# Two graph layers with their edge stages in a written-out order, and the router's and features' work laid beside other stages

## The chip, the cores and the metric

The kernel runs on one core of a Trainium2 chip. The metric is device time in microseconds (us) from launch to end, lower is better. A core has five engines that run side by side, each through its own queue in order: PE (matrix products, results into PSUM), DVE (vector work), ACT (activation functions and copies), POOL (here mostly gathers by index, which it issues as DMAs) and SP (plain DMAs). They wait for each other by semaphores.

## The reference

Two rounds over one graph of 3125 nodes (256 features) and 53,125 edges, each round followed by a feed-forward part. Cut to what matters:

```
x1 = layernorm(x);  feats[h] = x1 @ Ws[h] + bs[h]                      # 4 heads of 64
w  = exp(-relu((a_s[src] + a_d[dst] + aw_e*elem + ab) / 20))           # per edge, head
x += segment_sum(w * feats[dst], src) / segment_sum(w, src)            # edge stage 0
x2 = layernorm(x);  x += sum over the top 2 of 16 experts of p_e * expert_e(x2)
h  = layernorm(x);  score = h[src]@w_src + h[dst]@w_dst + rel[etype]@w_rel
al = exp(leaky_relu(score)); al = al / al
agg = segment_sum(((h[src] + rel[etype]) @ Wn) * al, dst)              # edge stage 1
x += relu(agg) + where(in_degree > 0, h @ loop_w, h @ evolve_w)
z  = layernorm(x);  wt = z @ wr + br                                   # one number per node
x  = x + z + (the 1561 nodes of highest wt: wt * (gelu(z@w1 + b1)@w2 + b2))
```

All products are in float32; indicator matrices are bf16 or f16.

## The kernel before, in words

The nodes are 25 tiles of 128. A sort in the kernel (`sort_edges`) puts the edges into 25 buckets by the node that receives, 18 tiles of 128 edges a bucket (8 in the last), 440 tiles in all. The sort for round 0 comes first; the ranking part of the sort for round 1 is a Python generator whose pieces are given as `fill` to edge stage 0, and its moves are spread over the experts.

An edge stage (`edge_stages`, run by `pipelined`) goes over 74 groups of up to 6 edge tiles, three groups to a bucket. `gather` lets POOL fetch a row of the table per edge into `rows` (L754), builds the one-hot `oh` of the receiving node (DVE, L762) and the transposed one-hots `hot` (DVE, L771) from `wide`, a bucket's row numbers broadcast to all partitions by a DMA on SP (L744). `message` multiplies `hot` by the nodes' own parts (PE, `ps_near`, L780; 6 products a group in stage 0, 18 in stage 1), adds the pieces (DVE, L787) and calls `messages`: in stage 0 two exponentials on ACT (L924, L925) and the product of weights and rows (DVE, L926); in stage 1 the edge's weight (L1310 to L1282), the relation's one-hot written beside the row (DVE, L1313) and six scaled copies of `oh` on ACT (L1319). `add` sums over the edges by products with `oh` into the bucket's PSUM half (PE, L798). At a bucket's end `acc` takes the sum plus `more`, loaded just then from DRAM (L804, L806), and `finish` ends the bucket: in stage 0 a division and the sum into `x` (L937 to L940), then `done`, which every five buckets normalizes and makes the gate's logits; in stage 1 four transposes and eight products on PE (L1330 to L1343), copies on ACT and seven operations on DVE.

The order of instructions on each queue is not the program's: the framework's planner reorders what stands in different steps by its own costs. Products of all kinds but the sums and the experts' hidden layer share the four PSUM buffers of `ps_b`.

After edge stage 0 come the experts (65 tiles of 128 rows, weights streamed per tile), the sum of the experts' results into `x` over 25 tiles with two gathers each (L1170, L1174), then `relations_features`: weights for the relations, layer norm of all tiles (`norm_tiles`), features of all tiles into `table1` (L1264 to L1270). Then edge stage 1, then `depths`: layer norm of all tiles, the score `wc`, its transposed copy `wrow`, the rank of every node by comparing with all others (49 comparisons, `cmp`, L1426), and the last feed-forward part tile by tile (L1445 to L1473).

Of the kernel before, what the change touches and what calls it, by code (L numbers as in the profile page):

```python
# [9 lines left out]
F32 = mybir.dt.float32  # L10
# [12 lines left out]
class _Kernel:  # L23
# [12 lines left out]
    def __init__(self, ctx, tc, a, out):  # L36
# [18 lines left out]
        for b in range(self.NT):  # L55
# [7 lines left out]
        assert self.MT % self.KB == 0  # L63
# [3 lines left out]
        self.psum = ctx.enter_context(  # L67
            tc.tile_pool(name="psum", bufs=1, space=bass.MemoryType.PSUM)
        )
# [5 lines left out]

    def ps_a(self, name):
        return self.psum.tile([P, 1024], F32, tag="A", name=name, bufs=2)

    def ps_b(self, name):
        return self.psum.tile([P, 512], F32, tag="B", name=name, bufs=4)  # L80
# [17 lines left out]
    def constants(self):  # L98
# [14 lines left out]
        iota_i = self.work.tile([P, 512], I32, name="iota_i", bufs=1)  # L113
        nc.gpsimd.iota(iota_i, pattern=[[1, 512]], base=0, channel_multiplier=0)
        self.iota = c.tile([P, 512], F32, name="iota")
        nc.vector.tensor_copy(self.iota, iota_i)
# [51 lines left out]
    def transposed(self, src, n, name, evac=None):  # L168

        nc, c = self.nc, n // P  # L170
        pt = self.ps_b(f"ps_{name}")
        for i in range(c):
            nc.tensor.transpose(pt[:, i * P : (i + 1) * P], src[:, i * P : (i + 1) * P], self.ident)  # L173
        dst = self.work.tile([P, c, P], F32, tag=f"T{c}", name=name, bufs=3)
        (evac or nc.scalar.copy)(dst.rearrange("p c q -> p (c q)"), pt[:, :n])  # L175
        return dst
# [133 lines left out]
    def sort_edges(self, pool, rp, name, seg, other, value, bits, tab, help, roomy):  # L310
# [23 lines left out]
        def load_in():  # L334
# [6 lines left out]
            yield  # L341
# [23 lines left out]
            yield  # L365

        def places():
# [4 lines left out]
            for b0 in range(0, NT, piece):  # L372
                m = min(piece, NT - b0)
                hot = tl([P, piece, EC], BF16, "hot", bufs=1)
                for b in range(b0, b0 + m):
                    eng = nc.vector if b % 3 == 0 else help
                    eng.tensor_scalar(hot[:, b - b0, :], bf, float(b), None, op0=OP.is_equal)
                    if b % 6 == 5:
                        yield
                hv = hot.rearrange("p b (s t) -> p b s t", t=C)  # L380
                for w, ps in ((self.ones_h, tot), (self.before_h, pre)):
# [5 lines left out]
                    yield  # L387
# [39 lines left out]
            yield  # L427
# [3 lines left out]
            for b in range(NT):  # L431
# [13 lines left out]
                yield  # L445
# [39 lines left out]
            for s in range(NS):  # L485
# [13 lines left out]
                if s % 3 == 2:  # L499
                    yield  # L500
# [77 lines left out]
        def load():  # L578
# [4 lines left out]
            wide = [self.dram.tile([MT, P], BF16, name=f"{name}_w{i}") for i in range(1 + (not bits))]  # L583
            with tc.tile_pool(name=f"{name}_back", bufs=1) as bp:
# [13 lines left out]
                def turned(v):  # L598
                    pt = self.psum.tile([P, 1024], F16, tag="B", name=f"{name}_pt", bufs=4)
# [13 lines left out]
                for i, w in enumerate(wide):  # L613
                    wb = bp.tile([P, nb, P], BF16, name=f"{name}_wb{i}")
                    nc.vector.tensor_copy(wb[:m], tk[:m, :, :, 1 + i])
                    nc.sync.dma_start(w.rearrange("(i k) p -> k i p", k=m), wb[:m])
# [107 lines left out]
    def edge_stages(self, pool, st, table, width, into, near, others, messages, W, sums, finish):  # L724
# [4 lines left out]
        nc, G = self.nc, self.GRP  # L729
        nv = near.shape[3]  # L730
        now = {}


        hold, sums2 = self.ps_a("ps_hold"), self.ps_a("ps_sums")
        numbers = hold[:, :256]
        nc.vector.tensor_copy(numbers, self.iota[:, :256])
        self.numbers, self.weights_ps = numbers, hold[:, 512:]

        def spread(i, b):

            t = pool.tile([P, self.tiles[0] // 2, 2 * P + 8], BF16, name=f"wide{i}")
            src = st["wide"][i][self.first[b] : self.first[b] + self.tiles[b], :]
            src = src.rearrange("(o k i) p -> o k (i p)", o=1, i=2)
            nc.sync.dma_start(  # L744
                t[:, : self.tiles[b] // 2, : 2 * P], src.to_broadcast([P, self.tiles[b] // 2, 2 * P])
            )
            return t

        def gather(g, b, k, n, head, last):
            if head:  # L750
                now[b] = [spread(i, b) for i in range(len(st["wide"]))]
            rows = pool.tile([P, G, into], F32, name="rows", bufs=3)
            for j in range(n):
# [5 lines left out]
                )  # L759
            sh = [P, n, P]  # L760
            oh = pool.tile([P, G, P], F32, name="oh", bufs=3)
# [4 lines left out]
            lo = (k - self.first[b]) // 2  # L766
            hots = []
            for i, (at, _) in enumerate([(self.pcol1, None)] + others):
                w = now[b][min(i, 1)][:, lo : lo + n // 2, : 2 * P]
                t = pool.tile([P, G // 2, 2 * P], BF16, name=f"hot{i}", bufs=2)  # L770
                nc.vector.tensor_scalar(t[:, : n // 2, :], w, at, None, op0=OP.is_equal)  # L771
                hots.append(t)
            return rows, oh, hots

        def message(g, b, k, n, head, last, rows, oh, hots):
            pe = self.ps_b("ps_near")
            picks = [near[:, b]] + [v for _, v in others]
            for j in range(n):
                for i, (t, v) in enumerate(zip(hots, picks)):
# [6 lines left out]
            own = pool.tile([P, G, nv], F32, name="near")  # L786
# [4 lines left out]
            return messages(k, n, rows, own, oh)  # L791

        def add(g, b, k, n, head, last, oh, msg):
            if head:
                now["sum"] = sums2[:, b % 2 * 512 : (b % 2 + 1) * 512]
            ps = now["sum"]
            for j in range(n):
                nc.tensor.matmul(  # L798
                    ps[:, :W], oh[:, j, :], msg[:, j, :],
                    start=(head and j == 0), stop=(last and j == n - 1),  # L800
                )
            if last:
                more = pool.tile([P, W], F32, name="more")
                nc.sync.dma_start(more, sums[b])  # L804
                acc = pool.tile([P, W], F32, name="acc")
                nc.vector.tensor_add(acc, ps[:, :W], more)  # L806
                finish(b, acc)

        return gather, message, add

    def pipelined(self, stages, fill=()):


        groups, done = self.edge_groups(), {}
        fill = iter(fill)
        for step in range(len(groups) + len(stages) - 1):
            if step > 2:
                next(fill, None)
            for i, stage in enumerate(stages):
                g = step - i  # L820
                if 0 <= g < len(groups):
                    done[g] = stage(g, *groups[g], *(done.pop(g, None) or ()))
        for _ in fill:
            pass
# [56 lines left out]
    def heads_edges(self, st, fill, done):  # L881
# [26 lines left out]
        with self.tc.tile_pool(name="edge0", bufs=2) as pool:  # L908
# [24 lines left out]
            def finish(b, acc):  # L933
# [7 lines left out]
                done(b)  # L941

            self.pipelined(self.edge_stages(
                pool, st, self.table0, W, W, near, [], messages, W, self.sums0, finish
            ), fill)
# [3 lines left out]
    def gate(self, pool):  # L949
# [16 lines left out]
        def done(b):  # L966
# [4 lines left out]
            self.norm_tiles(xn, t0, t1)  # L971
            nc.sync.dma_start(xv[:, t0:t1, :], xn[:, t0:t1, :])
            pl = self.ps_b("ps_logit")
            for t in range(t0, t1):
                xt = self.transposed(xn[:, t, :], D, "x_t")
                for c in range(C):
                    nc.tensor.matmul(
                        pl[:, (t - t0) * NE : (t - t0 + 1) * NE], xt[:, c, :], gw[:, c, :],
                        start=(c == 0), stop=(c == C - 1),
                    )  # L980
            nc.vector.tensor_tensor(
                self.logits[:, t0:t1, :],
                pl[:, : (t1 - t0) * NE].rearrange("p (t e) -> p t e", e=NE),
                self.gate_b[:, None, :].to_broadcast([P, t1 - t0, NE]), op=OP.add,
            )
# [3 lines left out]
    def experts(self, fill):  # L989
# [5 lines left out]
        with tc.tile_pool(name="moe", bufs=2) as pool:  # L995
# [143 lines left out]
            def turned(k):  # L1139
                w3, hid = live.pop(k)  # L1140
                live[k] = w3, self.transposed(hid, HID, "h_t")
# [25 lines left out]
            for t in range(NT):  # L1167
                for i in range(2):
# [8 lines left out]
                    )  # L1177

    def relations_features(self):
        nc, a, NT, D = self.nc, self.a, self.NT, self.D
# [13 lines left out]
        with self.tc.tile_pool(name="rel", bufs=2) as pool:  # L1196
            w3 = pool.tile([P, W3 // P, W3], F32, name="w3a", bufs=1)
            nc.sync.dma_start(w3, a["L1_gnn_W3"].rearrange("(c p) j -> p c j", p=P))
            av = pool.tile([P, W3], F32, name="av", bufs=1)
            self.row_bcast(av, a["L1_gnn_a"], W3)  # L1200
            wv = pool.tile([P, W3 // P], F32, name="wv", bufs=1)
            for c in range(W3 // P):
                nc.vector.scalar_tensor_tensor(
                    w3[:, c, :], w3[:, c, :], 1.0, av, op0=OP.mult, op1=OP.mult,
                    accum_out=wv[:, c : c + 1],
                )
# [48 lines left out]
            self.h1 = self.layer_norm("xn2")  # L1255
            t1v = self.table1.rearrange("(t p) c -> p t c", p=P)
            for t0 in range(0, NT, 5):
                f = pool.tile([P, 5, D + 2], F32, name="f1")
                n = min(5, NT - t0)
                for t in range(t0, t0 + n):  # L1260
# [8 lines left out]
                nc.vector.tensor_copy(self.near1[:, t0 : t0 + n, :], f[:, :n, D + 1 :])  # L1269
                nc.sync.dma_start(t1v[:, t0 : t0 + n, :], f[:, :n, : D + 1])  # L1270

    def relations_edges(self, st):
# [27 lines left out]
        with self.tc.tile_pool(name="edge1", bufs=2) as pool:  # L1300
# [7 lines left out]
            def messages(k, n, rows, near, oh):  # L1308
                s = pool.tile([P, 3, G], F32, name="s1")
                nc.vector.tensor_add(s[:, 0, :n], near[:, :n, 0], rows[:, :n, D])  # L1310
                weight(s[:, 1, :n], s[:, 0, :n], s[:, 2, :n])
# [4 lines left out]
                )  # L1316
                ow = pool.tile([P, G, P], F32, name="ohw", bufs=3)
# [6 lines left out]
            def finish(t, acc):  # L1324

                pt = self.ps_b("ps_cnt")
                rc = [(r0, min(P, R - r0)) for r0 in range(0, R, P)]
                ct = pool.tile([P, len(rc), P], F32, name="ct")
                for i, (r0, n) in enumerate(rc):
                    nc.tensor.transpose(  # L1330
                        pt[:n, i * P : (i + 1) * P], acc[:, R0 + r0 : R0 + r0 + n], self.ident
                    )
# [225 lines left out]
```

## Time and profile before

| | us |
|---|---|
| median of 3 runs | 2635.79 (2631.52 to 2639.92) |
| the profiled execution's own time | 2845.15 |
| its span | 2842.8 |
| PE, DVE, POOL, ACT busy | 1878.6, 1446.3, 1167.4, 390.7 |
| granted PE clock, mean | 0.822 |

The profiled execution is 209 us longer than the median of the runs, so a duration from the profile is one of that execution. In the profile a row names line, engine, operation and tile, its count, busy time and mean, and after the second bar the engine's idle time before it with what ended it. "issue" is an idle time for which the profile shows no wait; "remote" is a wait that ended with a signal that the profile ties to no recorded instruction. The ends of PE's products are modelled, not observed.

By their first and last instructions the stages are: first sort and features to 430 us, edge stage 0 from 430 to 1176, experts' choice to 1210, experts to 1717, their sum to 1790, features of round 1 and loading of the sorted edges to 1872, edge stage 1 to 2560, rank and feed-forward part to the end.

### The profile page before, as it was taken

How to read it: one execution, taken by the hardware profiler on the slowest of the kernel's cores; microseconds unless marked ns; L12 is line 12 of the kernel's file. 1: busy time of each engine (PE TensorE's matmuls, PEld its weight loads, DVE VectorE, ACT ScalarE, POOL GpSimd, SP SyncE). 2: the span in 40 equal slices, each digit the busy share in tenths (PEclk: the TensorE clock that was granted, in tenths of full speed). 3: DMA queues.
4: the chain of work that ended last, by engine and by line, in shares of the span. 5: the costliest groups of instructions: out<-in, count | busy, mean ns of one | idle time of the engine just before them, and what ended most of it. 6: DMA issues, size and time to landing. Idle time of an engine off the chain costs nothing.

```text
span 2842.8 us, 24381 instructions
## 1 busy us (share of the span) xinstructions
PE 1878.6 (66%) x7534; PEld 1126.4 (40%) x7534; DVE 1446.3 (51%) x3397; ACT 390.7 (14%) x1097; POOL 1167.4 (41%) x1198
## 2 busy tenths in 40 slices
PE   3169554854544443399999991447878778785298
PEld 0024232543433332356666660323434334343166
DVE  4876225476665343644422224445655556549721
ACT  0000010010000000100112120112222222221012
POOL 4235306576654646034411115036666666650000
PEclk9999996676666667577799996768889888898599
DMA  2000325343444433144499982254545455431000
GB/s 83 0 3 5 104 89 137 93 130 112 115 100 114 116 100 101 49 150 130 131 316 318 317 291 84 87 156 131 148 129 148 130 142 149 128 85 34 8 21 18
DMA packets 258938, 334.04 MB, mean 118 GB/s; under 512 B 30861, under 2 KB 192407, under 8 KB 258807
## 3 DMA queue, kind: packets, MB, share of 16 engines
q1 hardware_dynamic: 197527, 191.26, 21.3%
q0 software_dynamic: 51920, 132.68, 17.6%
q10 hardware_dynamic: 9360, 8.52, 0.9%
q8 instruction: 61, 1.00, 0.1%
q14 instruction: 70, 0.57, 0.1%
HBM read 298.38 MB, written 33.98 MB: 117 GB/s over the span
## 4 chain that ended last, share of the span: by engine, by line
PE 39%; DVE 14%; issue 10%; POOL 9%; another core or an unknown queue 8%; DMA 4%; ACT 1%; SPq 0%; DVEq 0%; POOLq 0%; ACTq 0%
PE ps_sums L798 10%; PE ps_h L1130 9%; POOL rows L754 9%; PE ps_y L1147 4%; PE s_mv L560 3%; DVE cmp L1426 3%; PE ps_hid L1453 3%; PE ps_out L1464 3%; DMA rows<-table,s_idx 3%; DVE msg L926 2%; DVE hot L771 2%; PE ps_x_t L173 1%; PE ps_h_t L173 1%; PE ps_f L1264 1%
## 5 line engine op out<-in xcount | busy, mean ns | idle before, releaser
L754 POOL DMA_INDIRECT rows<-table,s_idx x880 | 848.6, 964 | 725.0 <-issue 240.4
L798 PE MATMUL ps_sums<-msg,oh 128*128 128x260 f32 x880 | 306.6, 519 | 261.8 <-DVE msg L926 143.1
L798 PE MATMUL ps_sums<-rows,ohw 128*128 128x457 f32 x880 | 414.0, 616 | 62.8 <-ACT ohw L1319 54.1
L798 PEld LDWEIGHTS ps_sums<-msg,oh 128*128 128x128 f32 x880 | 226.6, 265 | 325.1 <-issue 250.1
L560 PE MATMUL s_mv<-s_hv,s_hp 128*128 128x200 f16 (+1 forms) x832 | 246.8, 472 | 89.9 <-DVE s_hv L555 89.9
L798 PEld LDWEIGHTS ps_sums<-rows,ohw 128*128 128x128 f32 x880 | 179.0, 215 | 217.5 <-issue 149.6
L1130 PE MATMUL ps_h<-w,x_t 128*128 128x512 f32 x520 | 256.1, 638 | 0.0
L771 DVE TENSOR_SCALAR hot<-wide,pcols 128x768 bf16<-128x768 bf16 (+1 forms) x296 | 175.4, 597 | 73.9 <-PE ps_near L780 63.0
L560 PEld LDWEIGHTS <-s_hp 128*128 128x128 f16 x832 | 122.1, 147 | 208.7 <-issue 180.3
L762 DVE TENSOR_TENSOR oh<-ps_hold,s_row 128x768 f32<-128x768 f32 (+1 forms) x148 | 139.9, 946 | 125.7 <-remote 73.5
L1119 POOL DMA_INDIRECT xg<-xtab,who x65 | 61.9, 952 | 345.1 <-PE ps_x_t L173 302.6
L569 POOL DMA_INDIRECT s_tab<-s_rec,s_to x130 | 147.8, 1137 | 115.1 <-ACT s_rec L566 78.9
L780 PEld LDWEIGHTS <-hot 128*128 128x128 bf16 x1760 | 70.0, 98 | 212.3 <-issue 149.2
L1136 DVE TENSOR_TENSOR hid<-hid,ps_h 128x512 f32<-128x512 f32 x65 | 44.7, 688 | 210.3 <-ACT hid L1135 204.4
L1319 ACT ACTIVATE ohw<-oh,s 128x128 f32<-128x128 f32 x440 | 136.5, 388 | 106.6 <-DVE s L1282 75.2
L1130 PEld LDWEIGHTS ps_h<-w,x_t 128*128 128x128 f32 x520 | 102.8, 209 | 105.7 <-issue 105.5
L926 DVE TENSOR_TENSOR msg<-rows,ps_hold 128x1536 f32<-128x1536 f32 x74 | 128.1, 1731 | 2.0 <-ACT ps_hold L924 1.9
L787 DVE TENSOR_REDUCE near<-ps_near 128x24 f32<-128x72 f32 (+2 forms) x148 | 29.4, 198 | 190.3 <-remote 150.2
L1147 PE MATMUL ps_y<-w,h_t 128*128 128x256 f32 x520 | 122.9, 379 | 0.7 <-ACT h_t L175 0.7
L1147 PEld LDWEIGHTS ps_y<-w,h_t 128*128 128x128 f32 x520 | 98.7, 190 | 41.7 <-issue 30.6
L545 DVE TENSOR_TENSOR s_hp<-num_p,s_pp 128x1024 f16<-128x1024 f16 x104 | 71.8, 690 | 82.8 <-PE s_mv L560 81.4
L1313 DVE TENSOR_TENSOR rows<-ps_hold,s_val 128x1200 f32<-128x1200 f32 x74 | 101.1, 1367 | 6.1 <-PE ps_sums L798 6.1
(307 smaller groups left out, 2344.2 us busy)
## 6 DMA issues: line engine op xcount, KB each, us to landing
w<-in_L_ffn_w_dram SPq DMA_DIRECT2D x195, 512.0 KB
wide<-s_w SPq DMA_DIRECT2D x72, 576.0 KB
rows<-table,s_idx POOLq DMA_INDIRECT x880
ytab<-y ACTq DMA_DIRECT2D x65, 128.0 KB
sums<-sums_z SPq DMA_DIRECT2D x5, 1142.5 KB
more<-sums SPq DMA_DIRECT2D x25, 228.5 KB
sums<-sums_z SPq DMA_DIRECT2D x5, 650.0 KB
table<-f SPq DMA_DIRECT2D x5, 650.0 KB
```

The costliest lines, as they stand in the source:

```text
L560: nc.tensor.matmul(ps[:, : NK * V], hp[:, :, j], rec[:, :, :, j].rearrange("p k v -> p (k v)"), start=(j0 + j == 0), stop=(j0 + j == C - 1),)
L569: d = nc.gpsimd.indirect_dma_start(out=tab, out_offset=bass.IndirectOffsetOnAxis(ap=to[:, i : i + 1], axis=0), in_=out[:, k * CH * V : (k ...
L754: nc.gpsimd.indirect_dma_start(out=rows[:, j, :width], out_offset=None, in_=table, in_offset=bass.IndirectOffsetOnAxis(ap=st["idx"][:, k + ...
L762: nc.vector.tensor_tensor(oh[:, :n, :], numbers[:, None, :P].to_broadcast(sh), st["row"][:, k : k + n, None].to_broadcast(sh), op=OP.is_equal,
L771: nc.vector.tensor_scalar(t[:, : n // 2, :], w, at, None, op0=OP.is_equal)
L798: nc.tensor.matmul(ps[:, :W], oh[:, j, :], msg[:, j, :], start=(head and j == 0), stop=(last and j == n - 1),)
L926: nc.vector.tensor_tensor(msg[:, :n, :HO].rearrange("p j (h o) -> p j h o", o=O), rows[:, :n, :HO].rearrange("p j (h o) -> p j h o", o=O), ...
L1130: nc.tensor.matmul(ph[:, i * HID : (i + 1) * HID], xt[:, c, :], w12[:, i, c, :], start=(c == 0), stop=(c == C - 1),)
L1147: nc.tensor.matmul(py[:, :D], ht[:, c, :], w3[:, c, :], start=(c == 0), stop=(c == HC - 1))
L1313: nc.vector.tensor_tensor(rows[:, :n, R0:], self.numbers[:, None, :R].to_broadcast(sh), st["val"][:, k : k + n, None].to_broadcast(sh), op ...
L1319: nc.scalar.activation(ow[:, j, :], oh[:, j, :], AF.Copy, scale=s[:, 1, j : j + 1])
L1426: nc.vector.tensor_scalar(cmp[:, s:e], wrow[:, s:e], w, None, op0=op, op1=OP.add, accum_out=rank[:, t, i : i + 1],)
```

## The change

- `edges` takes the place of `edge_stages` and `pipelined`. Its instructions stand in the program's order on every engine (`manual_schedule`). In step g: the row numbers of group g+2 are loaded, group g is gathered, bucket ends go on by a part, one-hots and `ps_near` of group g are made, then group g-1's near parts are read and its messages and sums are made, bucket ends go on by another part, and last comes a piece of other work from a queue (`piece(2.2)`, by nominal costs written at each `yield`).
- `ps_near`, the sums and `ps_hold` have PSUM buffers of their own (2, 2, 1); three are left for all else.
- `more` is loaded at a bucket's first group instead of its end. `wide` is loaded per group, 3 rows of 264 in one run per partition (1584 bytes) instead of 9 rows of 256 per bucket; `load` writes rows of that pitch. `rows` keeps 3 buffers in stage 0 and has 4 in stage 1, where `oh` goes from 3 to 2.
- The bucket's end in stage 1 is cut into four parts over three steps; the relation's one-hot is written in the gather's step (`prepare`).
- The work of `done` (gate) is cut into pieces. The norm, the score and the rank of the last part go into edge stage 1 as pieces (`router`): each group of up to five buckets is compared with those before it and itself, so there are 122 comparisons instead of 49, over as many columns in all.
- The weights for the relations are made ahead of the experts, and each tile's round 1 features follow as soon as its experts are summed, in groups of 4, at last 3 tiles.

```diff
-        for step in range(len(groups) + len(stages) - 1):
-            if step > 2:
-                next(fill, None)
-            for i, stage in enumerate(stages):
-                g = step - i
-                if 0 <= g < len(groups):
-                    done[g] = stage(g, *groups[g], *(done.pop(g, None) or ()))
+        with tc.manual_schedule():
+            spread(0)
+            spread(1)
+            for g in range(len(groups) + 3):
+                if g + 2 < len(groups):
+                    spread(g + 2)
+                if g < len(groups):
+                    rows = gather(g)
+                if g >= 3 and groups[g - 3][4]:
+                    closers.append(close(groups[g - 3][0]))
+                go_on()
+                if g < len(groups):
+                    live[g] = rows, *hots(g)
+                    if prepare:
+                        prepare(*groups[g][1:3], rows)
+                if 0 <= g - 1 < len(groups):
+                    message(g - 1)
+                go_on()
+                piece(2.2)
+            while closers:
+                go_on()
+            piece(1e9)
...
+                t = pool.tile([P, G // 2, 2 * P + 8], BF16, name=f"wide{i}", bufs=3)
+                src = w[k // 2 : (k + n) // 2, :].rearrange("(o k) r -> o (k r)", o=1)
...
+        def route(b):
+            if b + 1 not in ends:
+                return
+            i = ends.index(b + 1)
+            t0, t1 = ends[i - 1] if i else 0, b + 1
+            for _ in self.norm_pieces(z, t0, t1):
+                yield 1.2
...
+            for t in range(t0):
+                count(t, t0 * P, end, OP.is_gt, 3 + i)
+                if t % 3 == 2:
+                    yield 2.2
+            for t in range(t0, t1):
+                lo, hi = t * P, min(N, (t + 1) * P)
+                count(t, 0, lo, OP.is_ge, 0)
+                count(t, lo, end, OP.is_gt, 1)
...
+        general = dict(A=2, B=4)
+        at_edges = dict(near=2, sums=2, hold=1, B=3)
...
+                    self.rows_bufs, self.oh_bufs = 3, 3
                     self.heads_edges(st, ranking, self.gate(pool))
...
+                    features = self.relations_features()
+                    with tc.tile_pool(name="move1", bufs=1) as moves:
+                        self.experts([lambda f=f: f(moves) for f in steps], next(features))
+                        next(features, None)
+                    st = load()
+        with tc.tile_pool(name="route", bufs=1) as pool:
+            with self.banks(**at_edges):
+                self.router(pool)
+                self.rows_bufs, self.oh_bufs = 4, 2
+                self.relations_edges(st)
+            with self.banks(**general):
+                self.depths()
```

## The prediction

> **What bounds the kernel now.** No engine is busy over two thirds of the span, so I read the busy time by stretches first: start, length, then busy us (instructions) of PE, its weight loads, DVE, ACT, POOL, then PE's clock and the DMA share.
>
> ```profile
> 430.00:800.00 370.00, 209.64 (x856) 148.79 (x857) 231.93 (x547) 23.82 (x92) 236.38 (x234) 0.68 0.43 119
> 800.00:1176.00 376.00, 176.52 (x739) 135.45 (x737) 181.46 (x432) 28.39 (x100) 197.24 (x208) 0.68 0.37 98
> 1410.00:1710.00 300.00, 300.00 (x1125) 187.07 (x1124) 78.33 (x153) 60.29 (x102) 48.54 (x52) 0.99 0.91 301
> 1710.00:1800.00 90.00, 5.38 (x23) 3.65 (x21) 45.18 (x131) 2.78 (x4) 47.58 (x50) 0.56 0.36 111
> 1800.00:1870.00 70.00, 41.37 (x186) 29.46 (x186) 23.25 (x70) 9.30 (x25) 0.00 (x0) 0.87 0.17 56
> 1870.00:2200.00 330.00, 243.75 (x1166) 123.98 (x1166) 183.38 (x451) 80.22 (x272) 202.25 (x214) 0.84 0.54 146
> 2200.00:2560.00 360.00, 284.08 (x1327) 142.89 (x1326) 198.07 (x511) 92.01 (x316) 213.70 (x227) 0.88 0.47 126
> 2590.00:2685.00 95.00, 31.80 (x107) 20.89 (x108) 94.29 (x132) 8.40 (x12) 0.00 (x0) 0.67 0.01 3
> 2685.00:2843.00 158.00, 149.81 (x560) 100.98 (x559) 29.23 (x66) 35.15 (x58) 0.00 (x0) 0.99 0.05 19
> ```
>
> Edge stage 0 (first two rows, 746 us) has PE, DVE and POOL each near 55%: nobody is the bound, they wait in turn. Edge stage 1 (690 us) has PE at 76%. The experts are PE's and stay as they are. In 1710 to 1870 one engine works at a time; in 2590 to 2685 DVE alone; in the last row PE alone. Next, who waited for whom in stage 0 (us in total, times, longest), with one such wait in order of time (start, length, [idle before]):
>
> ```profile
> DVE oh L762 <- remote: 73.5, 9, 14.0
> DVE acc L806 <- remote: 70.8, 6, 18.4
> POOL rows L754 <- DVE msg L926: 161.5, 19, 23.6
> POOL rows L754 <- issue: 120.9, 397, 0.3
> ```
>
> ```profile
> 873.61 4.55 PE L798 MATMUL ps_sums<-msg,oh 128*128 128x260 f32 x12 [3.21 <-issue]
> 890.89 0.95 POOL L754 DMA_INDIRECT rows<-table,s_idx  x1 [0.30 <-issue]
> 895.90 0.43 DVE L806 TENSOR_TENSOR acc<-ps_sums,more 128x260 f32<-128x260 f32 x1 [16.00 <-remote]
> ```
>
> PE's record of the bucket's sums ends at 878.2, yet `acc`, which reads them, starts at 895.9; `more` for it was issued some 40 us earlier. So PE's product was signalled late (the modelled ends hide it), DVE stood with all its queue behind `acc`, freed no `rows`, and POOL stopped after filling its buffers. Such waits of DVE (`oh`, `acc`, 38.7 us more of `near`) make 183 us; 161.5 us of them reach POOL. Where the stage flows, POOL's gathers come every 0.95 + 0.30 = 1.25 us. In stage 1 PE is nearly closed:
>
> ```profile
> PE ps_near L780 <- issue: 56.1, 72, 1.9
> PE ps_sums L798 <- ACT ohw L1319: 54.1, 20, 2.8
> ```
>
> From 1885 to 2560 (675 us) PE is busy 526 us, and 85 us of its gaps are "issue" (these 56.1, and 20.1 and 8.6 before `ps_cnt` and the sums), which no reordering obviously removes. Only some 64 us are waits for others.
>
> **What the Trainium skill says.** "Perfetto Trace Analysis", section "Tensor Engine Instruction (MATMUL, LD_WEIGHTS)": the profiler computes a product's end and does not observe it; the 895.9 row agrees. "TensorE: Matmul & The Clock Gate", "What's actually happening": PE runs at half clock until it has been busy for a window. The trace agrees in direction: 0.68 in stage 0, 0.99 in the experts. "SBUF — State Buffer", "SBUF: two separate sides": DVE operations that take the shared port keep POOL from writing descriptors. The trace agrees: a gather takes 0.945 us on average in stage 1 and 0.983 in stage 0, where its longest is 1.55.
>
> **The change part by part**, in the time of the profiled execution.
>
> *Stage 0.* POOL's work stays: 440 gathers at 0.983 + 0.30 make 565 us, 7.7 a step. DVE's step in order: `hot` 0.60, `oh` 0.95, near 0.23, three small ones 0.55, a wait for ACT of about 0.35, `msg` 1.73, a bucket's end of 1.42 over three steps, together 4.9; the sort's piece (0.38 + 0.20 + 1.02 + 0.59 + 0.58) adds 2.8 in the first 40 or so steps. Consecutive DVE rows overlap by 0.1, so DVE needs 7.0 to 7.7: just under POOL. PE needs 385 us of 570. The wait is replaced by one step of slack: `near` is read a step after its products, `acc` two steps after the last sums, and `more` comes 18 tiles early. A lateness up to a step (7.7) is covered; longer ones (14 to 18 us, a handful) partly. New in DVE's strict order is that behind a late `near` stand the one-hots of the next step, which PE and ACT then wait for; I leave 20 us for these. SP issues 74 small `wide` loads at 0.36 us instead of 25; with two groups (15 us) of lead that is covered. So 565 + 15 until the first rows are used + 14 at the end + 20 = 614 against 746: **-132**.
>
> *Stage 1.* DVE: 372 us, plus two thirds of the router; the router's price: norm, score and equal-compare as now (8.2 + 15 + 8.7 + 7.8, some 40), comparisons 88.9 us for 49. The fastest took 0.277 us for 128 columns, the longest 3.47 for 3125: 1.07 ns a column and 0.14 fixed, with 0.09 for reading the sum. The 73 more comparisons cost 73 x 0.23 = 17, so 146 us, of which about 95 fall into the stage. DVE 467, POOL 440 x 1.245 = 548, PE 526 + 85 + the 25 transposes of scores (10) = 621 of 675: PE is the bound, and 8.4 us a step leave DVE's 7.7 room. SP's 148 loads and the weights that `router` now loads ahead of the stage lie beside work. **-53**. Below nothing is not excluded: a PE that rests less gets more clock; at 0.95 for 0.87 the 414 us of sums shrink by 35.
>
> *Features.* The sum over experts stays at 50 x 1.25 = 63 us of gathers, and DVE's added 25 x 1.43 = 36 us beside its 23 fit in. After the last sum (1790) there is now a norm of three tiles, three tiles of 1.87 each through PE, ACT and DVE, and the table's write: 16 us, where now the table is down at 1863. That is -57. The relations' weights (9.1 us of DMA, 5.4 + 6 of DVE) go ahead of the experts, where DVE is already busy 28 of 34 us: +12 on the path. **-45**.
>
> *End.* From 2560 to the end take 283 us now. After: the last two groups of `router` stay: for three tiles about 29 us of DVE (norm 8, 20 comparisons of 384 columns at 0.55, three of 2700 at 3.75 with company), for two tiles some 11 until their scores' copies are out, then PE can start on the feed-forward part (its buffers are handed over there); the remaining 20 of comparisons lie beside it. PE's part is 89.8 + 87.5 + 7.5 = 185, 5 to drain. 4 + 35 + 190 = 229: **-54**.
>
> The smaller edits (padded `wide` rows, two DMAs for one in `load`, `h_t` in another pool) I cost at nothing: `load` gains perhaps 2 us twice, the first `wide` (8.1 us for a bucket, seen before stage 1) comes sooner by more.
>
> Sum: -284, so the profiled execution of 2845 would become 2561. **Against the runs**: the profile is 209 us over their median, and the runs lie within 8.4 us of each other, which irregular waits of 14 to 18 us would hardly allow. So part of the late products probably is not in the runs. I take half of stage 0's gain, -66, between none and all, and the rest whole: -218, so 2635.8 - 218 = 2418, said as 2420.
>
> **The rivals.**
> 1. *The late products are in the runs as in the profile, and a steadier PE gets more clock.* For it: nothing in the records names the profiler; against it the narrow runs. -284 and up to -70: 2280 to 2370.
> 2. *The edge stages don't gain:* POOL paces stage 0 in the runs already (746 - 161 = 585, next to 565 of gathers) and PE stage 1. Only features and end: -99, or about 2535. For it: stretches such as 700 to 730, where a group took 6.9 us.
> 3. *Slower: strict order turns each late product or gather into a stop of all engines.* Place: DVE's queue in every step, `near` and the rows of g-1 ahead of the one-hots of g+1. Price: lateness beyond the step of slack. It decides from (66 + 53 + 99) / 148 steps = 1.5 us a step on; at 3 us a step it gives 2636 - 218 + 444 = 2860. Against it: gathers landed 2.5 to 5 us after issue in the chain of waits, and POOL has two more buffers to run ahead.
> 4. *The order isn't kept or changes nothing* (within 8 us of before): hardly possible with as many moved instructions.
>
> **How the numbers follow.** Forecast (2370 to 2500) 0.50, rival 1 0.22, rival 2 0.18, rival 3 0.08, rival 4 0.02. 0.3%, 8 us, is about what a measurement here can tell from no change. Faster is 0.90, same 0.02, slower 0.08. The range reaches from rival 1's all but lowest value to rival 2: 2270 to 2545.
>
> **What would show it.** In the profile after: DVE's remote waits in stage 0 under 60 us; POOL's gathers there 1.25 to 1.3 us apart with under 40 us of waits for `msg`; stage 0 near 615, stage 1 near 635 with PE busy over 80%; table 1 written within 20 us of the last expert's sum; feed-forward products within 40 us of the last bucket, without a stretch of DVE alone. It would be wrong if steps took 10 us with DVE waiting for `near` or rows in most of them, or if stage 0 were short in the profile and the runs gained under 110.

## The result, and the profile after

The changed kernel takes **2751.24 us** (median of 4 runs, 2750.01 to 2753.51) against 2635.78: ratio 1.0439, 95% interval 1.0421 to 1.0457, slower by 115 us. The prediction said 2420 and faster.

The profiled execution of the changed kernel takes 2753.51 us, like its other runs. That of before had been 209 us over its runs, so the two profiles, laid side by side, show the changed kernel 91 us *faster*. One more profile of the kernel before settled this: its own time was 2640.68, like its runs. In two of the five batches of experiments below the kernel before itself takes 2842 and 2845 us, with DVE's remote waits in the profiles of that batch, and in the other three 2635 to 2647 without them, so a ratio below is always to the kernel before of the same batch. By its time and its waits the first profile of before is like the two. Where the texts of the expectations speak of "the chip with late products", such a batch is meant, though one chip had a batch of each sort; that PE's products are what comes late is read from the waits, and why they would is open.

From here "before" is the second profile. The first view is DVE's waits in its edge stage 0, 429 to 1026 us (us in total, times, longest):

```profile
DVE s L919 <- DMA rows<-table,s_idx: 110.0, 32, 7.6
DVE near L787 <- PE ps_near L780: 35.0, 8, 7.6
DVE acc L806 <- PE ps_sums L798: 12.0, 8, 2.1
```

There is no remote wait left. DVE waits above all for gathered rows, so for POOL. By the first gather and the last `acc` of each edge stage, the spans divide so (us, to within 2; the last column is an experiment, told below, with the changed kernel's parts in the planner's order). All stage times from here on are of profiles without remote waits:

| | before | changed | planner's order |
|---|---|---|---|
| edge stage 0 | 597 | 649 | 587 |
| choice, experts, features, load | 692 | 674 | 666 |
| edge stage 1 | 636 | 763 | 572 |
| end | 284 | 235 | 216 |
| span | 2638 | 2751 | 2474 |

The changed kernel gained 67 us in the middle and at the end; the two edge stages lost 179. Busy time by stretches of the changed kernel (start, length, then busy us and instructions of PE, its weight loads, DVE, ACT, POOL, then PE's clock, DMA share, GB/s):

```profile
430.00:1077.00 647.00, 390.84 (x1585) 291.33 (x1586) 459.62 (x985) 50.81 (x190) 428.29 (x440) 0.72 0.46 126
1638.00:1762.00 124.00, 65.61 (x176) 42.25 (x177) 56.99 (x179) 12.18 (x33) 55.04 (x59) 0.52 0.39 119
1762.00:2516.00 754.00, 537.38 (x2501) 281.52 (x2497) 483.05 (x1180) 182.75 (x607) 411.15 (x433) 0.85 0.45 122
2516.00:2563.00 47.00, 8.05 (x24) 4.84 (x25) 40.72 (x113) 3.58 (x9) 0.00 (x0) 0.55 0.00 1
2563.00:2751.00 188.00, 180.18 (x669) 121.04 (x668) 49.87 (x129) 44.04 (x71) 0.00 (x0) 0.99 0.05 18
```

In edge stage 1 (third row) PE is at 71%, DVE at 64%, POOL at 55%: again nobody is the bound, and they wait in turn. For whom, waits of the changed kernel say, from 430 to 1077 (two lines) and from 1762 to 2516 (five):

```profile
DVE logits L1062 <- PE ps_logit L1059: 72.0, 23, 7.2
POOL rows L816 <- DVE msg L1002: 67.3, 15, 12.3
```

```profile
POOL rows L816 <- PE ps_sums L864: 144.9, 23, 9.2
PE ps_sums L864 <- ACT ohw L1412: 137.2, 58, 5.2
DVE agg L1447 <- PE ps_rel L1434: 124.3, 23, 6.3
DVE s L1372 <- ACT s L1371: 77.7, 73, 4.6
PE ps_near L844 <- DVE hot L830: 76.3, 82, 4.8
```

`agg` and `logits` read products of PE. In the second profile of before the same two reads wait little (1718 to 2354, and 429 to 1026):

```profile
DVE agg L1349 <- PE ps_rel L1336: 8.6, 12, 3.0
DVE logits L981 <- PE ps_logit L977: 5.7, 5, 3.0
```

One bucket's end of the changed kernel in order of time shows why (rows of PE and DVE; "..." marks rows left out):

```profile
2199.74 4.88 PE L864 MATMUL ps_sums<-rows,ohw 128*128 128x457 f32 x12 [1.10 <-ACT ohw L1412]
2204.46 1.03 PE L1434 MATMUL ps_rel<-rel_w,ct 128*128 128x257 f32 x4
2205.33 1.88 PE L1440 MATMUL ps_loop<-lw,x_t 128*128 128x512 f32 x4
2205.53 0.42 DVE L1447 TENSOR_TENSOR agg<-acc,ps_rel 128x256 f32<-128x256 f32 x1 [6.27 <-PE ps_rel L1434]
...
2208.16 1.64 DVE L830 TENSOR_SCALAR hot<-wide,pcols 128x768 bf16<-128x768 bf16 x3
2208.82 0.18 PE L844 MATMUL ps_near<-near1p,hot 128*128 128x3 bf16 x1 [1.62 <-DVE hot L830]
...
2213.71 6.60 PE L864 MATMUL ps_sums<-rows,ohw 128*128 128x457 f32 x12 [3.30 <-ACT ohw L1412]
```

`finish` issues `ps_rel` at the end of a step, behind that step's twelve products of sums (4.88 us); `agg` is the first thing that DVE does in the next step. So there is a step's *boundary* between them and no step. DVE stands 6.27 us, the next group's `hot` stands behind `agg`, and PE, done at 2207.2, waits for `hot`. ACT's scaled copies then come late, the sums start 3.30 us late, and `rows` is not freed for POOL.

### The profile page after: what moved, and what is told of

Read it like the earlier page. It is cut to its first block, busy times and chain, and to the rows that moved or that the text cites. A ratio compares the mean times of both kernels' runs of the same rounds, so it can differ in the third digit from the quotient of the medians.

```text
span 2751.4 us, 24818 instructions
## 1 busy us (share of the span) xinstructions
PE 1924.8 (70%) x7534; PEld 1165.0 (42%) x7534; DVE 1538.8 (56%) x3583; ACT 399.8 (15%) x1119; POOL 1165.6 (42%) x1198
## 5 line engine op out<-in xcount | busy, mean ns | idle before, releaser
L864 PE MATMUL ps_sums<-rows,ohw 128*128 128x457 f32 x880 | 418.9, 632 | 138.3 <-ACT ohw L1412 137.2
L864 PE MATMUL ps_sums<-msg,oh 128*128 128x260 f32 x880 | 325.6, 544 | 210.9 <-DVE msg L1002 205.0
L864 PEld LDWEIGHTS ps_sums<-msg,oh 128*128 128x128 f32 x880 | 237.3, 278 | 268.5 <-issue 211.6
L864 PEld LDWEIGHTS ps_sums<-rows,ohw 128*128 128x128 f32 x880 | 187.0, 220 | 322.1 <-ACT ohw L1412 170.3
L830 DVE TENSOR_SCALAR hot<-wide,pcols 128x768 bf16<-128x768 bf16 (+1 forms) x296 | 164.9, 598 | 6.2 <-DMA wide<-s_w 6.2
L1209 PEld LDWEIGHTS ps_h<-w,x_t 128*128 128x128 f32 x520 | 102.9, 209 | 105.8 <-issue 105.1
L844 PEld LDWEIGHTS <-hot 128*128 128x128 bf16 x1760 | 67.3, 98 | 186.6 <-DVE hot L830 150.5
L1002 DVE TENSOR_TENSOR msg<-rows,ps_hold 128x1536 f32<-128x1536 f32 x74 | 128.8, 1740 | 30.8 <-ACT ps_hold L1000 30.8
L1507 DVE TENSOR_SCALAR_CACHE_REDUCE cmp<-wrow,wc 128x640 bf16<-128x640 f32 (+16 forms) x122 | 107.1, 878 | 6.0 <-ACT wrow L1535 2.8
```

The costliest lines, as they stand in the source:

```text
L830: nc.vector.tensor_scalar(t[:, : n // 2, :], wide[g][min(i, 1)], at, None, op0=OP.is_equal)
L864: nc.tensor.matmul(bank[b][:, :W], oh[:, j, :], msg[:, j, :], start=(head and j == 0), stop=(last and j == n - 1),)
L1002: nc.vector.tensor_tensor(msg[:, :n, :HO].rearrange("p j (h o) -> p j h o", o=O), rows[:, :n, :HO].rearrange("p j (h o) -> p j h o", o=O), ...
L1209: nc.tensor.matmul(ph[:, i * HID : (i + 1) * HID], xt[:, c, :], w12[:, i, c, :], start=(c == 0), stop=(c == C - 1),)
L1507: nc.vector.tensor_scalar(cmp[:, s:e], wrow[:, s:e], wc[:, t : t + 1], None, op0=op, op1=OP.add, accum_out=rank[:, t, i : i + 1],)
```

## The experiments

Each edits the changed kernel, unless it says otherwise, and each median is of 4 to 12 runs (before's second profile: one). Batch 1 (the kernel before 2635.25) asked where the loss lies.

**The kernel before, profiled again.**

> The kernel before, unchanged, profiled once more. Theory L (the late PE products of the first profile, 183 us of DVE's remote waits in edge stage 0, belong to that one execution): the span is 2625 to 2650, DVE's remote waits in stage 0 are under 40 us, and stage 0 takes 560 to 600 us instead of 746. Theory P (a profiled execution of this kernel is always some 200 us longer than its runs): span above 2780 again, with the same waits in stage 0.

2640.68 us, stage 0 of 597 us, waits as shown above. Theory L holds: the 183 us of remote waits belong to the first profile and not to the kernel.

**Old stage 1** (`edge_stages`, `pipelined`, the old bucket's end and PSUM buffers; norm, score and rank after the stage), and **old stage 0** (the same for stage 0, with the old `done`). The old methods are put back whole; of the first edit only the calls are shown:

```diff
...
-            with self.banks(**at_edges):
-                self.router(pool)
-                self.rows_bufs, self.oh_bufs = 4, 2
-                self.relations_edges(st)
-            with self.banks(**general):
-                self.depths()
+        with self.banks(**general):
+            self.relations_edges(st)
+            self.depths()
```

> The changed kernel with edge stage 1 and the end (router after the stage) as in the kernel before; edge stage 0, experts and features stay changed. Theory A (in stage 1 DVE stands in its strict order at agg until PE's products are out, 124 us in the profile, and this is what made the change slower): 2640 to 2680, that is 70 to 110 below the changed kernel's 2751. Theory Z (stage 1 and the end are not worse than before, and the loss lies in edge stage 0, which in undisturbed executions took some 560 us before and takes 647 now): 2740 to 2770.

> The changed kernel with edge stage 0 and the gate's pieces as in the kernel before (a whole bucket's wide rows in one transfer, the bucket's end at once, planner's order); everything from the expert choice on stays changed. Theory A (the loss lies in stage 1): 2735 to 2765, about the changed kernel. Theory Z (the loss lies in stage 0): 2650 to 2680, 70 to 100 below the changed kernel. If both stages lose, 2700 here and 2690 in the run with the old stage 1.

Old stage 1: 2663.67 us (ratio to before 1.0105, 1.0088 to 1.0123). Old stage 0: 2694.83 (1.0226, 1.0209 to 1.0243). So both stages lose: undoing stage 0 gives back 56 us, and undoing stage 1 gives back 88, although it gives up the new end's 49. In the stages' own times the old stage 1 takes 637 us where the new takes 763, and the old stage 0 599 where the new takes 649.

**Half a step more before `agg`:**

```diff
                 yield
+                yield
                 xt = self.x[:, t, :]
                 v = pool.tile([P, D], F32, name="agg")
                 nc.vector.tensor_add(v, acc[:, :D], pr[:, :D])
```

> The changed kernel with half a step more between the products ps_rel and ps_loop and DVE's agg that reads them (one more yield in stage 1's finish; nothing else changes). Theory A: DVE's wait for ps_rel, 124 us in stage 1, falls under 30 us, PE's waits for hot fall with it, stage 1 goes from 754 to about 660, total 2650 to 2680. Theory W (the wait only moves to the next product, near, since PE is as late there): stage 1 stays over 730 and the total over 2730, with DVE's wait for ps_near in place of ps_rel.

**2636.63 us**, ratio to before 1.0003 (0.9995 to 1.0012): one `yield` takes back all 115 us. Waits of this kernel from 1755 to 2400:

```profile
DVE ln_rs L192 <- ACT ln_rs L190: 37.5, 4, 10.2
DVE agg L1448 <- PE ps_rel L1434: 14.4, 16, 2.5
...
PE ps_near L844 <- DVE hot L830: 27.5, 25, 4.7
```

`agg`'s wait goes from 124.3 to 14.4 us, PE's wait for `hot` from 76.3 to 27.5, and the stage from 763 to 645. Theory A holds, with some more gained than its range; the wait did not move to `near`.

Batch 2 met the late products (the kernel before 2841.87); batch 3 (2638.62) had three of its kernels again, beside the changed one.

**The logits a step later,** on top of the half step at `agg`. (The kernel before had one addition for all tiles of a group, as here; the change had split it into one behind each tile's product.)

```diff
-                    pl = self.ps_b("ps_logit")
+                    pl = pl or self.ps_b("ps_logit")
...
-                    nc.vector.tensor_add(self.logits[:, t - 1, :], pl[:, :NE], self.gate_b)
                 if t < t1:
                     yield 1.0
+            yield 2.2
+            nc.vector.tensor_tensor(self.logits[:, t0:t1, :], ..., op=OP.add)
```

> The changed kernel with the half step before agg, and in edge stage 0 the products of a group's logits in one PSUM tile with one DVE addition, a step after the last product, in place of an addition straight behind each tile's product. Theory G (DVE's 72 us of waits for ps_logit, 23 times 3.1 us, are what stage 0 lost against the kernel before): stage 0 goes from 650 to 585 to 605, the total from 2637 to 2575 to 2600. Theory H (the strict order as such costs the 52 us: each step's DVE work and its waits for ACT and rows are longer than a group's gathers, whatever logits do): the wait for ps_logit goes, but waits for rows, ps_hold or msg take its place, stage 0 stays over 635 and the total over 2620.

> Half a step before agg, and the logits added once for a group, a step after the last product; once more, since its first run fell on the chip with late products. If the kernel before takes 2636 here, theory G (72 us of waits for ps_logit are what stage 0 lost): stage 0 585 to 605, total 2575 to 2600; theory H (fixed order as such costs it): stage 0 over 635, total over 2620. If the kernel before takes 2842: 2814 again.

2814.14 beside 2841.87, and 2601.20 beside 2638.62 (0.9855, 0.9823 to 0.9886). The wait is gone and stage 0 falls from 650 to 609, so 41 of the 72 us of waits are gained; stage and total lie just outside theory G's ranges. A part returns as DVE's wait for ACT's `ps_hold` (59 us, before this edit 31). Theory H falls as the main cause.

**Old stage 0 with the half step at `agg`.**

> The changed kernel with the half step before agg, and edge stage 0 with the gate's pieces as in the kernel before. If the two costs add up (stage 0's order 56 us, the stop at agg 115 us): 2637 - 56 = 2581, from 2570 to 2592, faster than the kernel before by 2%. If they share something (clock, the expert choice): 2600 or more.

2829.19 (0.9927, 0.9895 to 0.9960), in batch 2 only. With late products it can't be told from the kernel with later logits; whether the two costs add up to 2581, as was expected without late products, stays untested.

**The planner's order:** the same parts, banks and pieces, without the fixed order.

```diff
-        with tc.manual_schedule():
+        if True:
```

> The changed kernel without the fixed order: the edge stages' instructions are the same, but the planner may order them as it did in the kernel before. Theory A (what cost time is the place of agg in DVE's fixed order): the planner moves other work ahead of agg and logits, both waits shrink to under a third, total 2600 to 2680. Theory N (the pieces themselves cost the time, whatever their order): within 20 us of 2751.

> The changed kernel with the edge stages in the planner's order instead of the fixed one. If the kernel before takes 2636 here, theory A (the place of agg and logits in DVE's fixed order costs the time): 2570 to 2650; theory N (the pieces cost it in any order): over 2700. If it takes 2842: 2800 again.

**2475.92 us** beside 2638.62: 0.9383 (0.9358 to 0.9407), the fastest of all and 274 us under the changed kernel; in batch 2, 2799.82 beside 2841.87. The 2476 is 94 us below the range of theory A, so `agg` and the logits are not all that the fixed order costs: with both mended in the fixed order the kernel took 2601, and the planner's order takes another 125 us off (by the profiles 22 in edge stage 0, 76 in edge stage 1, 20 at the end and 6 between).

The changed kernel beside it in batch 3 took 2750.21 (1.0426, 1.0401 to 1.0451):

> The changed kernel, unchanged, beside the others on one chip, because the kernel before took 2636 us on one chip and 2842 on another. If this chip is like the first: 2745 to 2757, with DVE's wait for ps_rel at 124 us. If it is like the second, where DVE's remote waits for late PE products appear in every profile: theory A says that the stop at agg adds to them, 2900 to 2960; the rival says that the added step of slack absorbs as much lateness as agg costs, 2830 to 2860, no slower than the kernel before there.

It has been run only where the kernel before takes some 2636 us, so what it does under late products is not known. Four rows of the planner's order, in edge stage 1, show what replaces the stop:

```profile
2104.66 0.15 DVE L1370 SCALAR_TENSOR_TENSOR s<-s 128x6 f32<-128x6 f32 x1
2104.73 0.87 DVE L1507 TENSOR_SCALAR_CACHE_REDUCE cmp<-wrow,wc 128x640 bf16<-128x640 f32 x1
...
2104.91 0.21 ACT L1371 ACTIVATE s<-s 128x6 f32<-128x6 f32 x1 [3.05 <-DVE s L1370]
...
2105.53 0.18 DVE L1372 RECIPROCAL s<-s 128x6 f32<-128x6 f32 x1
```

While ACT makes the exponential of `s`, DVE does a comparison of the router. DVE waits for this exponential 8 times, 2.7 us in all, against 73 times and 77.7 us in the changed kernel. What is left is POOL's: 72 us of DVE's waits are for gathered rows and the time behind them, and the stage's 440 gathers at 0.95 + 0.30 us make 550 of its 572 us (an estimate from these two durations).

**The router after edge stage 1** (on top of the half step at `agg`, and, two batches later, in the planner's order):

```diff
-                self.queue.append(self.route(t))
...
             with self.banks(**general):
+                for t in range(self.NT):
+                    for _ in self.route(t):
+                        pass
                 self.depths()
```

> The changed kernel with the half step before agg, and the router's pieces (norm, scores, comparisons) all after edge stage 1 instead of in its steps. Theory R (the router's 95 us of DVE work in the stage is hidden behind PE and POOL, as the prediction has it): stage 1 stays within 10 us of 645, the end grows by some 65 us to 300, total 2690 to 2710. Theory S (DVE's queue is what paces the stage in its fixed order, so the pieces lengthen it): stage 1 falls by 50 to 90 us, the end grows by 65, total 2615 to 2655.

> Half a step before agg, and the router's pieces all after edge stage 1. If the kernel before takes 2636 here: theory R (the router's DVE work in the stage is hidden) 2690 to 2710, stage 1 within 10 us of 645; theory S (DVE's fixed order paces the stage, the pieces lengthen it) 2615 to 2655, stage 1 at 580 to 610. The run on the other chip showed an end of 267 us, so 31 more than with the router in the stage, and not 65: with that, R gives 2665 to 2675 and S under 2635. If the kernel before takes 2842: 2829 again.

> The changed kernel in the planner's order, with the router's pieces after edge stage 1. In the fixed order the router in the stage cost the stage 66 us and saved 31 at the end. Theory F (the planner puts the comparisons into DVE's waits, so that they cost the stage next to nothing): stage 1 within 12 us of 572, the end 265 to 270 in place of 216, total 2515 to 2530. Rival (DVE's work paces the stage there too): stage 1 under 545, total under 2500.

> The planner's order with the router after edge stage 1. If the kernel before takes 2636 here: theory F (in the planner's order the router's comparisons fill DVE's waits) stage 1 within 12 us of 572, the end 265 to 270, total 2515 to 2530; rival (DVE's work paces the stage there too) stage 1 under 545, total under 2500. If it takes 2842: 2834 again.

In the fixed order 2597.84 beside 2638.62 (0.9845, 0.9825 to 0.9864; batch 2: 2829.18): the stage falls from 645 to 579, the end grows from 236 to 267 (against the half step at `agg` alone, of batch 1). The router *costs* 35 us there, net: theory S. In the planner's order, batch 5, 2525.09 beside 2647.43 (0.9537, 0.9508 to 0.9567): the stage is 564 in place of 572, the end 267 in place of 216 (the plain planner's order, batch 3). So there the router in the stage gains about 43 us: theory F. (Under late products, in batch 4: 2833.88 beside 2844.72.) DVE's work in the stage grows by 65 us in one case (419 to 484) and 58 in the other (400 to 458); it costs the stage 66 us in one order and 8 in the other. Edge stage 1 by busy time, in the fixed order with `agg` and logits mended:

```profile
1712.00:2360.00 648.00, 507.78 (x2508) 271.78 (x2508) 484.11 (x1178) 182.52 (x607) 417.88 (x440) 0.89 0.53 146
```

and in the planner's order:

```profile
1685.00:2258.00 573.00, 491.11 (x2505) 263.30 (x2506) 458.47 (x1198) 181.05 (x608) 416.99 (x440) 0.92 0.63 165
```

**A longer step after the norm's square root,** on top of half step and logits. A `yield` is not a step: `piece(2.2)` runs on while its budget lasts, so DVE's reciprocal was issued in the same step as ACT's square root.

```diff
         nc.scalar.activation(rs[:, :n], mv[:, t0:t1, 1], AF.Sqrt, bias=self.eps)
-        yield
+        yield 2.2
...
-            for _ in self.norm_pieces(z, t0, t1):
-                yield 1.2
+            for k in self.norm_pieces(z, t0, t1):
+                yield k or 1.2
```

> Half a step before agg, logits added a step later, and the router's and gate's norm pieces end their step after the square root on ACT, so that DVE's reciprocal comes a whole step later (before, several pieces run in one step while their budget of 2.2 lasts, and DVE waited 7 us for ACT each time). Relative to b_logit (2601). Theory D (in the fixed order DVE is closed: its work of 484 us in stage 1 and its waits in line add up, so each wait taken out is gained): ln_rs's 37 us go, stage 1 648 to 610 to 620, total 2565 to 2575. Rival (another engine closes the gap at once): total over 2590.

> Half a step before agg, logits a step later and the norm pieces' longer step, in the fixed order; its first run fell on the chip with late products. If the kernel before takes 2636 here: theory D (DVE is closed in the fixed order, its work and its waits in line add up) 2565 to 2580, stage 1 from 648 to 610 to 620; rival (another engine closes the gap) over 2590. If it takes 2842: 2791 again.

2570.59 beside 2647.43 (0.9720, 0.9692 to 0.9749), under late products 2790.81 beside 2844.72 (0.9793, 0.9732 to 0.9854). The stage falls from 648 to 620 and the 37 us of `ln_rs` are gone, so 28 of 37 us are gained: theory D. A part returns as DVE's wait for the exponential, 59.2 us before this edit (1712 to 2360); from 1700 to 2340 it is now its largest:

```profile
DVE s L1379 <- ACT s L1378: 81.5, 74, 7.3
```

The planner fills this wait; no run here aimed at it in the fixed order.

**The planner's order with all three mended steps, and the planner's order with `wide` fetched as rows of 512 bytes,** batch 4, under late products:

> The planner's order with the half step before agg, logits a step later and the norm pieces' longer step. Theory F (in the planner's order the written steps hardly matter, since a late operand is passed by): within 10 us of 2476. Rival (the planner follows the written order closely enough that the waits of the fixed order are there in part): 2430 to 2460.

> The planner's order, with the wide rows fetched without their padding, so as rows of 512 bytes instead of one piece for a group. The prediction costed this edit at nothing: within 8 us of 2476. Rival (the one-piece transfer leaves DMA time to the gathers): 2490 or more.

2787.04 (0.9783, 0.9738 to 0.9828) and 2808.21 (0.9834, 0.9782 to 0.9885), where the plain planner's order had had 0.9880 (0.9832 to 0.9928) in batch 2, on another chip. The second can't be told from it, and the first lies only just below it. The expectations are for batches without late products, in which neither ran, so both questions stay open. The fixed order with its three mends, 2790.81 in the same batch, equals the planner's order with the same mends here, while without late products it is some 90 us longer than the plain planner's order (ratios to before of 0.9720 and 0.9383, in two batches). That the written steps absorb late products where the planner's order doesn't would fit, but is only argued.

## Why the prediction was wrong, point by point

**The basis.** "Against the runs" was right to doubt the profile, and half right in what it did: of stage 0's 132 us it kept 66. The second profile shows that nothing of it was in the runs: before the change stage 0 takes 597 us, and the working ends at 614 after it. DVE's remote waits are gone there, and POOL's wait for `msg` is 17.7 us for 161.5. Rival 2 had this (585). The planner's order, which keeps the change's earlier `near` and `more`, gains 10 us.

**Stage 0: -66 predicted, +52 measured.** Besides the basis, the step that failed is "The wait is replaced by one step of slack". It is true of `near` and `acc` (waits of 9.3 and 1.3 us) and was taken to be true of the gate's pieces, which have no term at all in the sum of DVE's step. But a logit's addition stands in the same piece as its product: 72 us of waits, and 41 us came back with one later read.

**Stage 1: -53 predicted, +127 measured.** The failed step is the same, at `agg`, whose wait was put at nothing: the twelve sums and four products ahead of it on PE are the 6 us, once a bucket, and moving the one read gave 115 us. The second is the conclusion "PE is the bound" from a comparison of busy times (DVE 467, POOL 548, PE 621), by which the router's 95 us counted as covered. In a fixed order busy times don't say that: DVE's work came out at 484 us, near the 467, but its waits in line stand on top, nothing may pass them, and the router lengthened the stage by 66 us.

That the planner's order makes 636 into 572, -64, close to the -53, is luck. The sum went from 675 to 621 with 85 us of PE's "issue" gaps kept as unavoidable; these gaps are not among PE's waits in the second profile of before, and 572 lies 49 under the 621. What stands in their place (1718 to 2354) is

```profile
PE ps_cnt L1330 <- DVE acc L806: 106.9, 25, 6.0
```

PE's wait for `acc` ahead of the bucket's transposes. With the old stage 1 put back it is 105.8 us; with the bucket's end cut into parts it is 1.3 in the planner's order and absent in the fixed one. So the new stage removes it, and in the fixed order other waits take its place (137.2 us for `ohw`, above). That cutting the bucket's end alone gives the 64 us is argued: no run makes that edit alone.

**Features: -45 predicted, -18 measured.** The weights ahead of the choice cost some 12 us, as said (42 to 54). From the last gather of the experts' results to the first gather of the stage the time falls from 84 to 41 us: -44, for -57. The failed step is that DVE's and PE's share beside the sum over experts would "fit in": the sum takes 82 us for 65, and from the first expert's product to that last gather 574 for 560, +15. One term that the prediction put at nothing here is PE's clock. Spread over the sum, the same 100 products of the features take a median of 636 ns each, for 382 in one stretch before (clock 0.50 from 1661 to 1740, and 1.00 from 1658 to 1706), and a tile needs 3.03 us in turn where the prediction took 1.87.

**End: -54 predicted, -49 measured.** Its working holds in the main: PE's 188 us for 190, and 47 us of DVE alone for the 4 and 35 of the sum (29 and 11 in its text). The sign that there would be no stretch of DVE alone did not come true.

**Rivals.** Rival 3, at 0.08, was the right mechanism, a stop of all engines in DVE's strict order. It had the queue right (DVE's) and the reads wrong (`near` and the rows; they hold). It had the cause wrong too, *late* products: those that `agg` reads follow the sums on PE without a gap and were asked for too early. Its price fits: the fixed order cost 649 - 587 + 763 - 572 = 253 us, over 148 steps 1.7 us a step, past its point of 1.5. Had the order been left to the planner, 2418 would have been 58 us off.

**What would show it.** Of the signs named, remote waits under 60 us came true, but say nothing, since the kernel before has none in its second profile either. Stage 0 near 615, waits for `msg` under 40, and stage 1 near 635 with PE over 80% did not (649; 67.3; 763 with 71%). Of the signs of being wrong, steps of 10 us came in stage 1 (763 us over 74 groups), with DVE waiting for `agg` and not for `near` or rows.

## What to carry to other kernels

Before an order is fixed, write down for every read of another engine's result what stands *between* the issue and the read on both queues: a step's boundary, or a `yield` that may run on in the same step, is not a step. A sum of busy times by engine says what a stage could take if nobody waits in line; in a fixed order add each wait of the queue that feeds all others. And before a profile is priced, see that its own time agrees with the runs; if it doesn't, its largest waits are the first suspects.

## What the runs showed of the hardware

The same 2505 to 2508 products of edge stage 1 kept PE busy for 491 us at a mean clock of 0.92 in the planner's order (row above) and for 541 us at 0.84 in a second profile of the changed kernel:

```profile
1742.00:2506.00 764.00, 541.16 (x2508) 283.20 (x2508) 485.63 (x1186) 182.68 (x607) 417.18 (x440) 0.84 0.46 124
```

Busy time times clock is 452 and 455, so the 50 us go with the clock. The Trainium skill, "TensorE: Matmul & The Clock Gate", "What's actually happening", has the clock depend on PE being kept busy; the trace agrees in direction, down to single groups: the twelve sums behind the stop shown above take 6.60 us, those ahead of it 4.88. So a stop of PE costs its own length and then slower products.

- Work that is moved into the gaps of another stage can run slower there: the features' products went from 382 to 636 ns, and the clock from 1.00 to 0.50, when they were laid beside the sum over experts.
- POOL's gathers kept 0.95 to 0.99 + 0.30 us on average in every version. By this estimate 440 of them take 550 us in edge stage 1 and some 565 in edge stage 0, and 572 and 587 are near it. In the first profile all 59 gathers over 1 us lie in edge stage 0; that DVE's operations hold them up, as the prediction reads the trace, was not tested.
